# The first layer of a four-layer network, rewritten as pipelines of two batches

## The chip, the cores and the metric

The kernel runs on one core of a Trainium2 chip. The metric is the time of one execution on the device in microseconds; lower is better. The engines are called as in the profile: PE (TensorE, matmuls; PEld are its weight loads), DVE (VectorE), ACT (ScalarE), POOL (GpSimd) and SP (SyncE, which here only issues DMAs). Everything is computed in 32-bit floats.

## The reference

A residual stream x of 8 batches of 512 tokens and width 128 runs through four layers. Each layer is a half feed-forward, an attention and the same half feed-forward again, each with a layer norm in front:

```
x = x + 0.5 * ffn(layernorm(x));  x = x + attn(layernorm(x));  x = x + 0.5 * ffn(layernorm(x))
```

The change is in layer 0. Its feed-forward is a mixture of 8 experts for 4096 tokens: softmax over 8 logits (router weights), the two largest kept, 7 experts with a capacity of 512 tokens each (the first 512 in token order; relu between a 128x512 and a 512x128 matrix), and the eighth a copy of the input times its weight. Its attention works inside segments of 32 tokens without heads (scores over all 128 columns, scale 1/sqrt(8)). Beside it the first tokens of the 16 segments of a batch attend to one another; their result is added to every token of its segment before the output matrix:

```
fused = softmax(Q K^T * scale) V  +  softmax(Qg Kg^T * scale) Vg  (one row for a segment)
out   = fused @ wc.T + bc
```

Layer 1's feed-forward (the spline step, with an own norm inside) opens the next layer, and the change also moves how it starts. Layers 2 and 3 have small feed-forward weights that are worked out inside the kernel from 8 gathered matrices (l2_ffn_weights) and from the products of 8 pairs of matrices (l3_ffn_weights).

## The kernel before

x lives in SBUF, 8 tiles of 128 x (4 x 128), one for each batch of 512 tokens. Layer 0 goes stage by stage, each over all eight batches:

1. norm: stats takes bn_stats and bn_aggr of all 32 pieces on DVE, one square root on ACT and a refinement on DVE; DVE scales all pieces (L190), PE turns them (L193), ACT copies them (L194).
2. router (L330), the two largest and the routing table: the rank of each token within its expert comes from matmuls with triangular matrices, and the table of which token sits in which row of which expert from one-hot products on DVE (L440 to L443, four chunks of eight tiles) and PE (L445). The table goes through seven small DMAs (L453) to give src and dst, the row numbers for gather and scatter.
3. The experts: POOL issues indirect DMAs that gather rows of xn from DRAM (fetch, L489) and scatter the results to DRAM (put, L493); PE transposes, multiplies (L505, L513), ACT and DVE apply relu and copy. POOL's order is written by hand: put(e - 2) and fetch(e) in turns. yd, where the results go, is filled with zeros at the start of the kernel, from ACT's DMA queue.
4. back: the two result rows of each token are read from yd (r) and added with their weights on DVE (L539).
5. l3_ffn_weights and l2_ffn_weights work out later layers' weights.
6. l0_attn: norm again, projections of all batches (L564, L575), the summary attention for all batches, then per batch scores (L619), softmax_t, the local product (L626), its sum with the summary (L629), the output matrix (L634) and the addition to x.
7. norm, router, table, experts once more, and then back through l1_start.

l1_start is a pipeline with places: plan and a dictionary todo put each step of a batch at a place n, and the steps are then emitted in order of place; within tc.manual_schedule the order on the engines that it names is the order of emission, and each engine's queue is worked off in that order. A place is not a time: an engine goes on to its next instruction as soon as that one's inputs are there. Engines that are not named (POOL and SP in most places) are ordered by the framework's scheduler. In l1_start the norm of each batch is measure (bn_stats on DVE, then some 13 small operations on POOL with a power of -0.5) and four scalings on ACT (L833), followed by turned (four transposes on PE and a copy on ACT), and the steps of layer 1's feed-forward for batches 0 and 1, from place 13 and from place 33. whiten is measure plus four scalings on POOL (L231). The attention of layer 1, l1_block, follows; its projections (L909) need the turned batch 0 at the end of l1_start, and its buffers are cleared on POOL (L881, L884, L889).

## Time and profile before

| | us |
|---|---|
| median of 3 runs | 3029.14 (3025.25 to 3033.32) |
| profiled execution, its own time | 3021.69 |
| profiled execution, its span from first to last instruction | 3019.9 |
| PE busy | 2626.2 (87%) |
| DVE busy | 1985.9 (66%) |
| ACT busy | 1691.9 (56%) |
| POOL busy | 839.8 (28%) |
| mean granted PE clock | 0.92 of full |
| layer 0 and the start of layer 1 (to the first projection of layer 1) | 621.5 |

The busy times are of one execution and sum an engine's instructions, whatever waited for them. A busy PE is not PE at its peak: a matmul at half clock is busy for twice as long. Waits are listed by who waited and whose end released it; a wait at an engine that is not needed costs nothing. Which engine sets the pace is to be read stage by stage, since layer 0 is made of stages with different limits and the other layers are long pipelines.

### The profile page before, as it was taken

The numbers are of one execution on the slowest core, as the hardware profiler recorded it, in microseconds if no ns is written. First come the engines' busy times: TensorE is split into PE (matmuls) and PEld (weight loads), VectorE is DVE, ScalarE is ACT, GpSimd is POOL, SyncE is SP. The second block draws the span as 40 slices with busy tenths as digits, with TensorE's granted clock in tenths as the row PEclk, the third lists the DMA queues.
The fourth block names the chain that finished last, engine by engine and source line by source line (L and its number), as shares of the span: only waits on it lengthen the run. The fifth ranks groups of instructions, "written<-read, shape, count | busy, mean of one in ns | idle before, by whom it ended". The sixth has DMA issues, their size and how long they took to land.

```text
span 3019.9 us, 50759 instructions
## 1 busy us (share of the span) xinstructions
PE 2626.2 (87%) x18608; PEld 1512.7 (50%) x18608; DVE 1985.9 (66%) x5383; ACT 1691.9 (56%) x4102; POOL 839.8 (28%) x1783
## 2 busy tenths in 40 slices
PE   3637665669999999889999999999999999999997
PEld 3425543323334333456565565565555555555554
DVE  5345542458888877354756656655578888888886
ACT  1002101405555555566666665666488888888884
POOL 0433035722222233134254353351221011100100
PEclk9877577559999999899999999999999999999998
DMA  5031002100100000000000000000000000000000
GB/s 181 27 94 47 29 21 68 36 15 17 24 21 19 16 16 2 32 1 1 1 1 1 1 1 1 1 1 1 15 15 2 19 15 19 5 19 19 16 5 8
DMA packets 65863, 62.92 MB, mean 21 GB/s; under 512 B 9544, under 2 KB 55760, under 8 KB 63920
## 3 DMA queue, kind: packets, MB, share of 16 engines
q1 hardware_dynamic: 58144, 42.75, 5.5%
q10 hardware_dynamic: 3344, 8.99, 0.8%
q0 software_dynamic: 4128, 7.94, 0.8%
q8 instruction: 148, 2.42, 0.3%
q14 instruction: 99, 0.81, 0.1%
HBM read 36.83 MB, written 22.87 MB: 20 GB/s over the span
## 4 chain that ended last, share of the span: by engine, by line
PE 60%; DVE 14%; ACT 9%; POOL 8%; issue 5%; DMA 4%; SPq 0%; POOLq 0%; DVEq 0%; ACTq 0%
PE s L1080 8%; PE tp L1112 7%; PE s L934 5%; PE o L964 4%; PE yp L300 4%; PE o L1369 4%; PE o L1132 4%; PE s L1320 3%; ACT e L1327 3%; PE tp L1346 3%; DVE nm L935 3%; PE s L954 2%; PE pp L1289 2%; PE op L1383 2%; PE vp L1302 2%
## 5 line engine op out<-in xcount | busy, mean ns | idle before, releaser
L1084 DVE TENSOR_REDUCE nm<-s 128x2 f32<-128x1024 f32 x256 | 312.8, 1222 | 105.6 <-PE s L1080 105.2
L935 DVE TENSOR_REDUCE nm<-s 128x2 f32<-128x1024 f32 x256 | 307.6, 1219 | 105.9 <-PE s L954 82.6
L1091 ACT ACTIVATE e<-s,nm 128x512 f32<-128x512 f32 x512 | 350.4, 702 | 29.4 <-DVE nm L1084 29.4
L956 ACT ACTIVATE pr<-s 128x512 f32<-128x512 f32 x512 | 274.4, 600 | 143.6 <-PE s L954 142.8
L204 POOL TENSOR_TENSOR d<-st 128x4 f32<-128x4 f32 x88 | 17.9, 204 | 1200.4 <-DVE rs L1097 600.6
L1120 ACT ACTIVATE p<-tp 128x512 f32<-128x512 f32 x512 | 275.5, 608 | 71.1 <-PE tp L1112 69.1
L954 PE MATMUL s<-q,k 32*128 32x512 f32 x1024 | 309.7, 638 | 3.7 <-DVE at L977 2.3
L934 PE MATMUL s<-k,q 32*128 32x512 f32 x1024 | 290.5, 671 | 25.8 <-DMA k<-sk 14.3
L1080 PE MATMUL s<-k,q 32*128 32x512 f32 x1024 | 291.9, 648 | 4.8 <-ACT e L1091 2.4
L1112 PE MATMUL tp<-cst,e 128*128 128x128 f32 x2048 | 287.0, 282 | 5.8 <-DVE e L1104 5.0
L1327 ACT ACTIVATE e<-e,m 128x512 f32<-128x512 f32 (+3 forms) x512 | 285.6, 568 | 8.1 <-DVE m L1324 8.0
L1112 PEld LDWEIGHTS tp<-cst,e 128*128 128x128 f32 x2048 | 220.9, 142 | 136.8 <-issue 100.6
L1324 DVE CUSTOM_DVE_ANT_0 e<-s,bias 128x512 f32<-128x512 f32 (+3 forms) x512 | 219.9, 486 | 99.9 <-PE s L1320 99.4
L1348 ACT COPY pt<-tp 128x512 f32<-128x512 f32 x320 | 173.7, 588 | 100.7 <-PE tp L1346 100.3
L1104 DVE TENSOR_SCALAR e<-e,rs 128x512 f32<-128x512 f32 x448 | 201.9, 487 | 9.1
L303 DVE SCALAR_TENSOR_TENSOR x<-yp,sel,x 128x128 f32<-128x128 f32 x512 | 178.4, 349 | 22.6 <-PE yp L300 8.2
L231 POOL TENSOR_SCALAR xn<-x,sm,rs 128x128 f32<-128x128 f32 x232 | 188.7, 824 | 6.2
L1320 PE MATMUL s<-qk 64*128 64x512 f32 (+3 forms) x1024 | 174.6, 460 | 2.3 <-DVE m L1324 1.6
L1346 PE MATMUL tp<-cst,e 128*128 128x128 f32 x1280 | 169.1, 278 | 1.7 <-ACT e L1327 1.7
L1346 PEld LDWEIGHTS tp<-cst,e 128*128 128x128 f32 x1280 | 141.4, 142 | 41.6 <-issue 16.1
L1377 DVE TENSOR_TENSOR att<-o,rt 128x512 f32<-128x512 f32 x64 | 44.3, 692 | 173.3 <-ACT rt L1376 173.3
L934 PEld LDWEIGHTS s<-k,q 32*128 32x128 f32 x1024 | 88.2, 193 | 132.6 <-DVE nm L935 74.9
(423 smaller groups left out, 4816.3 us busy)
## 6 DMA issues: line engine op xcount, KB each, us to landing
r<-yd SPq DMA_DIRECT2D x32, 256.0 KB
yd<-zero ACTq DMA_DIRECT2D x4, 1024.0 KB
xd<-xn SPq DMA_DIRECT2D x16, 256.0 KB
k<-sk SPq DMA_DIRECT2D x64, 64.0 KB
sk<-pu SPq DMA_DIRECT2D x16, 256.0 KB
w<-in_l_w SPq DMA_DIRECT2D x14, 256.0 KB
q<-sq SPq DMA_DIRECT2D x32, 72.0 KB
x<-in_x SPq DMA_DIRECT2D x8, 256.0 KB
```

The costliest lines, as they stand in the source:

```text
L934: nc.tensor.matmul(s[:, jj, :], lhsT=q[cut, g, i * P : (i + 1) * P], rhs=k[cut, g, :], start=True, stop=True)
L935: nc.vector.tensor_reduce(nms[b, g // 2][:, i, 2 * h : 2 * h + 2, g % 2], s, AX.X, ALU.max, negate=True)
L954: nc.tensor.matmul(s, lhsT=k[cut, g, kt * P : (kt + 1) * P], rhs=q[cut, g, :], start=True, stop=True)
L956: nc.scalar.activation(e, s, AF.Exp)
L1080: nc.tensor.matmul(s[:, jj, :], lhsT=q[cut, g, i * P : (i + 1) * P], rhs=k[cut, g, :], start=True, stop=True)
L1084: nc.vector.tensor_reduce(nm, scores[n, h], AX.X, ALU.max, negate=True)
L1091: nc.scalar.activation(e, s[:, jj, :], AF.Exp, bias=nm[:, jj : jj + 1], accum_out=sm[:, jj : jj + 1])
L1112: nc.tensor.transpose(tp[:, kt, :], probs[n][j][:, kt * P : (kt + 1) * P], self.ident)
L1120: nc.scalar.activation(p, tp, AF.Exp)
L1320: nc.tensor.matmul(s[:, jj, 0:w], lhsT=qs[n][cut, i * P : (i + 1) * P], rhs=ks[n][cut, 0:w], start=True, stop=True)
L1327: outs.append(lambda e=e, jj=jj: nc.scalar.activation(e, e, AF.Exp, bias=mins[n][:, jj, i : i + 1], scale=-1.0, accum_out=sums[n][:, jj, i ...
L1346: nc.tensor.transpose(tp[:, k, :], block(n, jj, i, kt), self.ident)
```

## The change

Layer 0 is written anew as l0_block, five stretches with the order of PE, ACT and DVE written by hand:

- **Start**: four pairs of batches, pair(g) at place 6g. A pair is a measure of two batches together (POOL's small operations on 8 columns instead of 4), and for each of the two a scaling on ACT 7 places later, turned 3 places after that, and logits one after that. The choice of the two largest is made in two halves (chosen).
- **Table and experts**: the one-hot work in eight chunks of four tiles; the zeros for yd are written from SP's queue, from a tile cleared on POOL, behind the table in program order. Fetches run three experts ahead, put(e) comes after expert e, and fetch(e + 3) goes in turns with it. An expert is split in turn, inner and outer, with turn(e + 1) between inner(e) and outer(e). Beside the first pass of experts the eighth expert's part is added to x, and layer 3's products and layer 2's sums are made in pieces between the experts; layer 2's gathers are issued ahead of the first table, with their small loads on ACT's queue.
- **Middle**: returned results are loaded and added batch by batch, 10 places apart; pair(g) is measured at place 20g + 13, its attention begins at 20g + 34, and its second norm, with the router's logits, at 20g + 49. From the first addition to the last logits a pair takes 62 places, and a pair starts every 20.
- **Attention**: wv and wc are multiplied once to one matrix (wvc), so that there is no output matmul: leave accumulates the local product and, through a 0/1 matrix own, the summary's row of each segment straight into the output. The biases bv and bc are added to x as one row, bc + 2 bv wc. The softmax works on the unscaled scores, with the scale in the exponential. The summary is made per pair.
- **Second table and experts**, as the first, without the weights beside them.
- **Start of layer 1**: additions 4 places apart, pairs at 8g + 6, and the feed-forward steps of batches 0 and 1 side by side, two places a step, from places 20 and 21; whiten(0) at 55 and its transposes at 61.

stats, norm, router, l0_ffn, l0_attn and l1_start are gone. l3_ffn_weights and l2_ffn_weights return lists of steps. Layers 1 to 3 are as before. The core of the diff:

```diff
-            self.norm(ps)
-    def norm(self, ps, tag="mm", bufs=None):
...
+    def pair(self, todo, g, n, bank, gap, *also):
+        nc, got = self.nc, []
+        def scale(k):
+            (nb, rs), b = got[0], 2 * g + k
+            for i in range(4):
+                t = 4 * k + i
+                nc.scalar.activation(self.xn[b][:, i, :], self.x[b][:, i, :], AF.Identity, bias=nb[:, t : t + 1], scale=rs[:, t : t + 1])
...
+        at(n, lambda: got.append(self.measure([self.x[2 * g], self.x[2 * g + 1]], True)))
+        for k in range(2):
+            b = 2 * g + k
+            at(n + gap + 2 * k, lambda k=k: scale(k))
+            at(n + gap + 3 + 2 * k, lambda b=b: self.turned(self.xn[b], bank, self.xt[b]))
+            for delay, work in also:
+                at(n + gap + 3 + 2 * k + delay, lambda b=b, work=work: work(b))
...
+                for k in range(8):
+                    ts = slice(4 * k, 4 * k + 4)
...
-            with tc.manual_schedule(engines={mybir.EngineType.Pool}):
-                for e in range(9):
-                    if e < 7:
-                        for s in range(4):
-                            if e >= 2:
-                                put(e - 2, s)
-                            fetch(e, s)
-                        expert(e)
...
+                with tc.manual_schedule(engines={*FIXED, mybir.EngineType.Pool}):
+                    for e in range(3):
+                        for s in range(4):
+                            fetch(e, s)
+                    turn(0)
+                    for e in range(7):
+                        inner(e)
+                        if e < 6:
+                            turn(e + 1)
+                        outer(e)
+                        for s in range(4):
+                            put(e, s)
+                            if e + 3 < 7:
+                                fetch(e + 3, s)
+                        for k, work in enumerate(beside):
+                            if k * 7 // len(beside) == e:
+                                work()
...
+                def leave(k):
+                    x, op = self.x[2 * g + k], bank("op", (P, 4, P))
+                    for i in range(4):
+                        s0 = 16 * k + 4 * i
+                        nc.tensor.matmul(op[:, i, :], lhsT=box["own"][:, 32 * s0 : 32 * s0 + P], rhs=soft["go"], start=True, stop=False, skip_group_check=True)
+                        for j in range(4):
+                            rows = slice(32 * j, 32 * j + 32)
+                            nc.tensor.matmul(
+                                op[rows, i, :], lhsT=soft[k][rows, 32 * i : 32 * i + 32], rhs=vs[k][rows, i, :], start=False, stop=True, skip_group_check=True)
+                    nc.vector.tensor_tensor(x, x, op, ALU.add)
+                for k in range(2):
+                    at_(n + 2 * k, project, k, 0)
+                    at_(n + 2 * k, project, k, 1)
+                    at_(n + 2 * k + 1, values, k)
+                    at_(n + 3 + 2 * k, score, k)
+                    at_(n + 4 + 2 * k, powers, k)
+                    at_(n + 6 + 2 * k, divide, k)
+                    at_(n + 10 + 2 * k, leave, k)
+                at_(n + 4, summary)
+                at_(n + 5, powers, 2)
+                at_(n + 7, divide, 2)
+                at_(n + 9, spread)
...
+                    for g in range(4):
+                        self.pair(todo, g, 6 * g, bank, 7, (1, logits))
+                    chosen(todo, 0, 20)
+                    chosen(todo, 1, 33)
...
+                    w2, more = self.l2_ffn_weights(self.keep, pool)
...
+                    table(wk)
+                    z = wk.tile([P, 4, 512], F32, tag="h", name="z")
+                    nc.gpsimd.memset(z, 0.0)
+                    for n in range(4):
+                        nc.sync.dma_start(out=self.yd[2048 * n : 2048 * n + 2048, :].rearrange("(p n) d -> p (n d)", p=P), in_=z.rearrange("p a b -> p (a b)"))
...
+                    experts(wk, ps, [weights, *(work for works in zip(parts, steps, more(ps)) for work in works), more(ps)[8]])
...
+                    for b in range(NB):
+                        at(todo, 10 * b - 20, load, b)
+                        at(todo, 10 * b, add, b, 0)
+                        at(todo, 10 * b + 2, add, b, 1)
+                    for g in range(4):
+                        n = 20 * g + 13
+                        self.pair(todo, g, n, bank, 7)
+                        attention(todo, g, n + 21, wk, ps, bank)
+                        self.pair(todo, g, n + 36, bank, 7, (1, logits))
+                    chosen(todo, 0, 84)
+                    chosen(todo, 1, 123)
...
+                    experts(wk, ps, [weights] + [lambda b=b: self_part(b) for b in range(NB)])
...
+                    for b in range(NB):
+                        at(todo, 4 * b - 16, load, b)
+                        at(todo, 4 * b, add, b, 0)
+                        at(todo, 4 * b + 1, add, b, 1)
...
+                        self.pair(todo, g, 8 * g + 6, bank, 6, (1, lambda b, heads=heads, hts=hts: hts.__setitem__(b, heads[b % 2][0](self.xt[b]))),
+                                  (3, lambda b, heads=heads, hts=hts: heads[b % 2][1](hts[b])))
+                    for b in range(2):
...
+                        n = 20 + b
+                        self.plan(todo, [n + 2 * k for k in L1F_TAIL], *self.l1_ffn_steps(b, w1, bank, twin, self.xn[b], self.xt[b]))
+                    n = 21 + 2 * L1F_TAIL[-1]
+                    self.plan(todo, (n, n + 6), lambda _: self.whiten(0, self.xn[0]), lambda xn: self.turned(xn, bank, self.xt[0]))
```

## The prediction

> **What bounds the kernel now.** I read the busy times cut by stage first, with the cuts put where one stage hands over to the next in the timeline: start, first routing table, first experts, the stretch with the attention (the middle), second table, second experts, the start of layer 1, and the rest. Columns: window, length, busy time (instructions) of PE, PEld, DVE, ACT, POOL, then the granted PE clock, DMA share and GB/s.
>
> ```profile
> 0.00:61.30 61.30, 21.66 (x96) 19.15 (x96) 28.22 (x140) 7.89 (x12) 4.01 (x10) 1.00 0.70 223
> 61.30:99.20 37.90, 19.72 (x74) 16.03 (x74) 30.62 (x70) 0.00 (x0) 0.00 (x0) 0.93 0.01 1
> 99.20:198.30 99.10, 66.78 (x308) 41.44 (x308) 14.53 (x21) 12.46 (x21) 54.76 (x56) 0.84 0.11 37
> 198.30:372.20 173.90, 101.68 (x884) 82.03 (x884) 107.15 (x415) 27.23 (x56) 23.38 (x41) 0.63 0.22 64
> 372.20:409.60 37.40, 19.48 (x74) 15.87 (x74) 30.81 (x70) 0.00 (x0) 0.00 (x0) 0.73 0.01 0
> 409.60:511.30 101.70, 66.04 (x308) 41.09 (x308) 14.53 (x22) 12.46 (x21) 54.51 (x56) 0.85 0.12 41
> 511.30:621.50 110.20, 56.49 (x168) 33.89 (x168) 60.95 (x197) 38.56 (x79) 67.81 (x169) 0.50 0.16 49
> 621.50:3019.90 2398.40, 2274.38 (x16696) 1263.24 (x16696) 1699.08 (x4453) 1593.27 (x3913) 635.35 (x1451) 0.97 0.04 10
> ```
>
> The first seven rows are layer 0 with the start of layer 1: 621.5 us in which no engine is busy for more than 67% of a window but DVE in the tables (81%). The last row is not touched by the change and has PE busy for 95%. So the change can win or lose only in 621.5 us, by overlap. The waits and the timeline say why each window is as long as it is:
>
> ```profile
> 14.39 11.84 ACTq L390 DMA_DIRECT2D yd<-zero  x4
> 27.56 0.23 ACT L171 ACTIVATE sd<-ve 128x32 f32<-128x32 f32 x1
> ...
> 117.58 1.00 POOL L493 DMA_INDIRECT yd<-y,dst  x1 [8.35 <-ACT y L515]
> ...
> POOL x L635 <- DVE xn L190: 41.5, 7, 37.4
> PE pp L1475 <- DVE st L166: 37.0, 1, 37.0
> ACT xt L194 <- PE pt L193: 36.2, 12, 15.3
> ...
> ACT xn L833 <- POOL sm L220: 21.1, 2, 19.1
> ```
>
> At the start ACT is held for 11.84 us issuing the zeros, so the square root runs at 27.56 though its input was there at 18.3. In the experts the POOL queue, which issues all gathers and puts, stands still for 8.35 us until the first result. In the middle PE waits 37.0 us in one piece while DVE adds and measures all eight batches, and ACT, POOL and PE each wait for the whole stage ahead. Before layer 1 ACT waits 19.1 us for a norm on POOL, which was then clearing layer 1's buffers (L881 to L889).
>
> **The Trainium skill.** "TensorE: Matmul & The Clock Gate", Part 1: the PE clock is halved unless the array has been busy for a window of about 3.4 us. The trace agrees and adds that small matmuls don't count for much: clock 1.00 at 262 to 288 in dense projections, 0.50 at 295 to 385 though PE was busy for 93% of 300 to 325. "SBUF — State Buffer", SBUF: two separate sides: DVE operations with two SBUF inputs and POOL operations lock each other out. The trace agrees: eight L539 additions took 2.2 us with POOL idle (208 to 220) and 3.57 us at 524.6 with POOL at work. "ScalarE: Activation LUTs", What ACT_TABLE_LOAD costs: each switch of set costs a load; the trace has 1283 ns each.
>
> **The change, stage by stage** (window before to window after).
>
> *Start, 61.3 to 51.* Removed: the root, its table load, 32 aggregates (0.17 us), 32 DVE scalings; the zeros leave ACT. Added: four norms of two batches, each 8 statistics on DVE (0.22 us in a row, 1.8), 13 POOL operations (4.1 us for four columns at 530.06 to 534.15; eight columns are not shown, bounds 4.1 and 5.5, I take 4.6), and on ACT 4 scalings (1.65) and a copy (0.59) a batch. PE needs 1.1 + 1.9 = 3.0 a batch for transposes and logits at half clock. If the first statistics start at 5 (x lands at 4.7), PE begins at 5 + 1.8 + 4.6 + 1.7 = 13 and ends after 8 x 3.0 = 24 at 38; the second half of the choice, 20 operations of 0.31 on 128 columns and an exponential, takes 6.7: 45. If DVE must first do layer 1's weights, whose data land at 14.1 (L662), all is 11 later: 56. I take 51.
>
> *Tables, 37.9 to 37 and 37.4 to 34.5.* Cutting the one-hot work into 8 chunks (2.06 us of DVE each, by halving L443, L440, L441) lets PE start 2 us earlier and end 1.6 after DVE instead of 3.3; the self parts that DVE mixed in are gone. That is 3 us each. In the first, 5 small DVE operations and a matmul for the fused weights come ahead of it: +2. SP gets the four zero transfers (11.84 us of issue on ACT before) ahead of or beside the table's v transfers: nothing if they go early in the 37 us, up to +12 if they are queued in front; I take 0. The nine gathers of l2_ffn_weights (1.3 us each on POOL) lie in the same idle 37 us; their four loads on ACT have the choice in front of them as cover.
>
> *Experts, 99.1 to 95 and 101.7 to 94.* Three experts are fetched ahead, so the loop no longer waits for put before fetch. Start to first put stays 19. Then POOL: four rounds of put and fetch of 8 x 1.28 = 10.3, three of puts alone at 2.5 (each waits for the one before, 1.5 us in the trace) = 10: 71, + 2.2 to land = 92. PE per expert: 3.9 + 0.8 + 4.1 = 8.8, under POOL's 10.3, in the second pass: 92 to 96. In the first pass each expert also carries a layer 3 product (1.13, eight in all) and some 4 DVE additions: 10.0 to 11.5, so either may bound: 92 to 102.
>
> *Middle, 173.9 to 145.* What leaves: layer 3 and layer 2 weights, 25 us almost bare (222 to 250). PE work per batch, at half / full clock: two sets of transposes 2.2 / 1.6; q and k 3.0 / 2.0 (0.744 at L909, 1.98 for four at L564); values 2.05 / 1.1; scores 0.66 / 0.4; leave, 8 matmuls on own (0.256 / 0.135) and 32 small ones (a quarter of that if four run side by side as L964's do, half as bound) 4.1 / 2.2, up to 6.1; logits 1.9 / 1.1. Sum 13.9 / 8.4, and 1.2 / 0.7 a pair for the summary: 116 / 70 in all. DVE: per pair 16 additions 4.6, two norms 3.5, softmax 3.1, leave 1.4, summary 1.8, gaps 1.6 = 16; with the first choice 70 in all. ACT 13.6 a pair, 54. POOL 13 a pair, 52. PE sets the pace. It starts at 2.7 (first return, 198.3 to 200.98) + 4.6 + 1.8 + 4.6 + 1.7 = 15.5, and in front of the last logits waits once for an addition, a norm and a scaling, 9. With 116: 15.5 + 116 + 9 + 6.7 for the choice = 147; with 70 and 10 more in the first pair: 111. A third warm gives 135; 10 for PE standing in its fixed order behind a younger pair's transposes makes 145. A pair takes 62 places and starts every 20, so three do overlap.
>
> *Start of layer 1, 110.2 to 102.* The two spline chains go side by side instead of 20 places apart. DVE: 32 for both chains, 8 x 2.7 additions, 7 norms; PE 60 at half clock. First scores at 29, DVE-bound to 72, then on POOL two whitenings of 7.5 and a third for batch 0, additions and transposes: 100. POOL's clearing (6 x 1.8, 8 DMA issues of 0.55) moves and may land in front of that last whitening, +15, or wholly beside it; 2 for it.
>
> Sum after: 51 + 37 + 95 + 145 + 34.5 + 94 + 102 = 558.5, that is 63 less than 621.5. Against the profiled execution (3021.7, of which 3019.9 span) that is 2959; the median of the runs shown is 7.4 above this execution, so the forecast is **2966**. Layers 1 to 3 keep their 2398.4, give or take 5.
>
> **Rivals.**
> 1. *PE stays warm in the middle.* For: the projections and values of a pair are 8 us of dense matmuls, and 4.9 us of transposes were enough at 255. Against: logits and small products kept it at 0.50 for 90 us. Middle 111: 2932. Chance 0.23.
> 2. *Small gain.* DVE starts behind layer 1's weights (+5), zeros queued in front of the table (+12), clearing on POOL in front of the last whitening (+13): 2996. For: all three are placed by the scheduler, and the stall of 19.1 us shows the last. Chance 0.20.
> 3. *Slower: the written order makes PE and DVE take turns in the middle.* Each place is fixed on three engines; if leave waits for a softmax that stands on DVE behind additions waiting for r, and DVE then waits for PE, their times add: 15.5 + 116 + 70 + 9 + 6.7 = 217, 72 more than I take, 3038. It decides from a middle of 208 us. Against: ten places lie between values and leave. Chance 0.12.
> 4. That pairs don't overlap, since PE is full with two: this is the forecast's own cold case, 2968.
>
> **Numbers.** Forecast 0.45. A measurement here can tell 0.3% (9 us) from no change. Faster: forecast, rival 1 and most of rival 2: 0.84; same 0.05; slower 0.11. The range: below, rival 1 with the early start (2932 less 6) and the experts' good ends (less 6), rounded to 2915; above, rival 2 with the experts' bad end, 3012.
>
> **What would show it.** Right: PE's first transposes at 11 to 15; no ACT issue of zeros; POOL pairs of put and fetch without a break after the first 18 us of experts; middle 135 to 155 with PE busy for over 70% of it and DVE under 60%; in layer 1's start no wait of ACT for POOL over 8. Wrong: a middle over 170, PE waiting for DVE in many pieces of 1 to 3 us there, or layer 1's first projection over 110 after the last put.

## The result, and the profile after

Not faster but slightly slower: **3036.35 us** (median of 18 runs, 3030.52 to 3040.17) against 3028.85 us (18 runs) for the kernel before on the same chip, a ratio of 1.0021 (95% interval 1.0014 to 1.0027). The forecast was 2966, with a range to 3012. The profiled execution took 3030.52 us with a span of 3028.6, 8.7 more than before.

The busy times of the kernel after, cut where one stage hands over to the next, as they were for the kernel before (window, length, busy time and count of PE, PEld, DVE, ACT, POOL, granted PE clock, DMA share, GB/s):

```profile
0.00:59.80 59.80, 24.10 (x100) 20.41 (x100) 19.67 (x90) 18.69 (x44) 20.15 (x66) 1.00 0.72 226
59.80:96.30 36.50, 20.45 (x74) 15.29 (x74) 23.21 (x45) 0.00 (x0) 9.90 (x9) 0.95 0.17 46
96.30:199.80 103.50, 70.22 (x374) 49.08 (x374) 28.05 (x73) 14.58 (x29) 54.92 (x56) 0.83 0.22 67
199.80:374.40 174.60, 114.52 (x826) 70.96 (x826) 69.90 (x262) 51.73 (x118) 50.08 (x145) 0.59 0.13 37
374.40:409.20 34.80, 18.64 (x72) 14.05 (x72) 22.37 (x42) 0.00 (x0) 0.00 (x0) 0.79 0.01 0
409.20:507.90 98.70, 62.44 (x308) 41.38 (x308) 25.30 (x61) 12.17 (x21) 54.77 (x56) 0.79 0.14 42
507.90:623.70 115.80, 54.00 (x168) 34.06 (x168) 60.99 (x202) 34.03 (x76) 62.62 (x128) 0.51 0.16 46
623.70:3028.60 2404.90, 2277.51 (x16696) 1263.62 (x16696) 1696.34 (x4447) 1594.06 (x3914) 631.18 (x1437) 0.97 0.04 10
```

| stage | before | forecast | after | after less forecast |
|---|---|---|---|---|
| start, to the first mask | 61.3 | 51 | 59.8 | +8.8 |
| first table | 37.9 | 37 | 36.5 | -0.5 |
| first experts | 99.1 | 95 | 103.5 | +8.5 |
| middle | 173.9 | 145 | 174.6 | +29.6 |
| second table | 37.4 | 34.5 | 34.8 | +0.3 |
| second experts | 101.7 | 94 | 98.7 | +4.7 |
| start of layer 1, to its first projection | 110.2 | 102 | 115.8 | +13.8 |
| the rest | 2398.4 | 2398.4 | 2404.9 | +6.5 |

The column of differences sums to 71.7. So the question is not one loss but where five stages lost what they were to gain, and why a part that was not touched got longer. Four things are to be seen in the trace.

At the start POOL works on two pairs in turns, with a clearing between (timeline of POOL; start, duration, instruction, in brackets the idle time before it and its releaser):

```profile
10.08 0.25 POOL L170 TENSOR_TENSOR d<-st 128x8 f32<-128x8 f32 x1 [7.24 <-DVE st L167]
...
12.37 1.80 POOL L700 MEMSET z<- 128x2048 f32 x1
...
16.32 3.28 POOL L176 TENSOR_TENSOR r<-ve,half 128x8 f32<-128x8 f32 x2
...
20.83 0.37 POOL L185 TENSOR_TENSOR sm<-sm,rs 128x8 f32<-128x8 f32 x2
```

The first measure begins at 10.1, since a pair waits for its second batch of x, and ends at 21, which is 11 us later and not 4.6: its steps alternate with those of pair 1 (every "x2" is one of each), and the 1.8 us memset of the zeros' source lies in between.

In the middle, what PE waited for (total, times, longest; 33.3 of the first row is the wait for the stage to begin). vp L635 is the summary attention, which works on firsts, the first token of each segment, copied together by POOL; gp L646 (spread in the code) makes the summary's rows, for which leave then waits; pt are the transposes of a norm, lp the logits:

```profile
PE pt L225 <- ACT xn L207: 41.1, 2, 33.3
PE vp L635 <- POOL firsts L595: 14.6, 4, 7.0
PE lp L392 <- ACT xt L227: 7.6, 8, 1.8
PE gp L646 <- DVE t L629: 4.7, 1, 4.7
```

The tail of layer 0, on POOL: the last whitening, which the first transposes of layer 1 wait for, alternates with the clearing of layer 1's buffers and takes from 605.1 to 622.5; PE stands for 36.0 us in front of those transposes (from 584.2).

```profile
603.34 1.80 POOL L966 MEMSET q<- 128x2048 f32 x1 [1.73 <-issue]
605.11 0.20 POOL L170 TENSOR_TENSOR d<-st 128x4 f32<-128x4 f32 x1
...
605.55 1.80 POOL L969 MEMSET k<- 128x2048 f32 x1
...
611.37 1.05 POOL L176 TENSOR_TENSOR r<-ve,half 128x4 f32<-128x4 f32 x1
...
619.39 3.14 POOL L196 TENSOR_SCALAR xn<-x,sm,rs 128x128 f32<-128x128 f32 x4
```

And 600 us further on, in layer 1, ACT has a hole that the kernel before doesn't have:

```profile
1238.66 0.33 ACTq L1586 DMA_DIRECT2D wp<-in_l_attn  x1
1239.04 0.60 ACT L1041 ACTIVATE pr<-s 128x512 f32<-128x512 f32 x1 [7.43 <-DVE bq L1591]
```

ACT does exponentials for layer 1 there. In the order of its queue the load of a weight of layer 3 (wp) comes next, and it is issued only at 1238.66. What ended the wait is a DVE instruction behind the last step of a spline (1237.8 to 1238.5); my reading is that wp's tile lies in memory that this spline still uses, which no run shows by itself. PE then waited 6.9 us for ACT.

### The profile page after: what moved, and what is told of

Same layout as the page of the kernel before. It is cut to its first block, busy times and chain, and to the rows that moved or that the text cites. A ratio compares the mean times of both kernels' runs of the same rounds, so it can differ in the third digit from the quotient of the medians.

```text
span 3028.6 us, 50809 instructions
## 1 busy us (share of the span) xinstructions
PE 2641.9 (87%) x18618; PEld 1508.9 (50%) x18618; DVE 1945.8 (64%) x5220; ACT 1725.3 (57%) x4202; POOL 883.6 (29%) x1896
## 4 chain that ended last, share of the span: by engine, by line
PE 55%; DVE 9%; ACT 8%; POOL 5%; issue 2%; DMA 0%; POOLq 0%; ACTq 0%; DVEq 0%
PE s L1165 8%; PE tp L1197 7%; PE s L1019 5%; PE o L1049 4%; PE yp L286 4%; PE o L1459 4%; PE o L1217 4%; PE s L1410 3%; ACT e L1417 3%; PE tp L1436 3%; DVE nm L1020 3%; PE s L1039 2%; PE pp L1379 2%; PE op L1473 2%; PE vp L1392 2%
## 5 line engine op out<-in xcount | busy, mean ns | idle before, releaser
L170 POOL TENSOR_TENSOR d<-st 128x4 f32<-128x4 f32 (+1 forms) x96 | 19.9, 207 | 1272.9 <-DVE st L167 672.4
L1019 PE MATMUL s<-k,q 32*128 32x512 f32 x1024 | 291.2, 671 | 22.1 <-DVE nm L1020 11.5
L1414 DVE CUSTOM_DVE_ANT_0 e<-s,bias 128x512 f32<-128x512 f32 (+3 forms) x512 | 219.9, 486 | 99.0 <-PE s L1410 98.5
L225 PE MATMUL pt<-cst,xn 128*128 128x128 f32 x360 | 81.4, 347 | 156.1 <-ACT xn L207 99.0
L1410 PE MATMUL s<-qk 64*128 64x512 f32 (+3 forms) x1024 | 174.6, 460 | 2.6 <-DVE m L1414 1.9
L1436 PEld LDWEIGHTS tp<-cst,e 128*128 128x128 f32 x1280 | 141.4, 142 | 41.6 <-issue 16.1
```

The source lines that it names most:

```text
L1019: nc.tensor.matmul(s[:, jj, :], lhsT=q[cut, g, i * P : (i + 1) * P], rhs=k[cut, g, :], start=True, stop=True)
L1410: nc.tensor.matmul(s[:, jj, 0:w], lhsT=qs[n][cut, i * P : (i + 1) * P], rhs=ks[n][cut, 0:w], start=True, stop=True)
L1436: nc.tensor.transpose(tp[:, k, :], block(n, jj, i, kt), self.ident)
```

## The experiments

Times are given as ratio to the kernel before in the same comparison, since the chips differed: the kernel before took 3021.6, 3024.4, 3036.0 and 3023.6 us in the four comparisons. The kernel after stands at 1.0021. Stage lengths are from the profiles; layer 2, the same code in all, took between 921.8 and 935.1 us in them, so that only the stage that an edit touches is compared.

### Layer 3's loads off ACT's queue

```diff
-        nc.scalar.dma_start(out=self.wp, in_=a["l3_attn"])
+        nc.sync.dma_start(out=self.wp, in_=a["l3_attn"])
```
(and the same for wv)

> The kernel after the change, with layer 3's two weight loads wp and wv (L1586, L1588) issued on SP's queue instead of ACT's. Between the last scores of layer 1 (1206.3 us) and the first scores of layer 3 (2190.7 us) the changed kernel is 10 us longer than the one before, though the code there is the same. Theory: ACT stands for 7.4 us at 1231.6 to 1239 in front of the issue of wp, whose memory is only free when DVE has added the spline result (1238.5); PE then waits 6.9 us for ACT and runs cold for 12 us. With the issue on SP the wait is nobody's: time falls by 8 to 10 us, to about 3027, and the waits of ACT for DVE bq and of PE for ACT pr (6.9 us) are gone. Rival: PE and ACT are held there by the spline chain itself (DVE and POOL) and the issue only shows the wait: no change (within 2 us).

Measured: 1.0009 (1.0000 to 1.0018). The waits are gone, and layer 1 takes 639.8 us from its first projection to layer 2's first instead of 645.1 (before: 638.1). The theory holds for the wait; of the 8 to 10 us that it promised 5.3 show in layer 1, and 3.6 in the ratio. In every kernel here with this edit layer 1 took 635.2 to 640.5 us, in every other one made from the changed kernel 645.1 to 651.0. The change had left that code as it was; that the places of tiles in memory made the wait is argued, not shown.

### Layer 1's clearing off POOL

```diff
-                nc.gpsimd.memset(q, 0.0)
+                nc.vector.memset(q, 0.0)
...
-                    nc.gpsimd.dma_start(out=k[32 * j + 8 : 32 * j + 9], ...)
+                    nc.sync.dma_start(out=k[32 * j + 8 : 32 * j + 9], ...)
```

> The kernel after the change, with layer 1's clearing taken off POOL: the six memsets of q, k and va (1.8 us each) on DVE, the eight k<-in_one transfers on SP. Theory: at 603 to 623 us POOL alternates between the 13 small steps of the last whitening (batch 0) and this clearing, so that the whitening takes 20.3 us (605.1 to 622.5) with PE, ACT and DVE idle; alone such a measure takes 4.2 us and the four scalings 3.1. First projection of layer 1 then comes about 10 to 12 us earlier (610 to 614 instead of 623.7), time 3025 to 3028. Rival: the start of layer 1 is set by the rope table and the q, k buffers, which have to be loaded and cleared after the spline work has given its memory back (603.3), so that the first scores (641.1) do not move by more than 3 us and the time neither.

Measured: 1.0004 (0.9994 to 1.0013). The start of layer 1 takes 100.3 us instead of 115.8, and the first scores come at 628.7 instead of 641.1. That is what the theory asked for (its 605.1 to 622.5 are 17.4 us, not 20.3); the whole run shows about 5 us of it.

### Dense work in front of leave

```diff
                     for i in range(4):
                         s0 = 16 * k + 4 * i
+                        for _ in range(3):
+                            nc.tensor.matmul(op[:, i, :], lhsT=wa[:, 0, :], rhs=wa[:, 1, :], start=True, stop=True, ...)
```

> The kernel after the change, with three additional 128 x 128 x 128 f32 matmuls (of the q and k weights, results thrown away by the next matmul) ahead of each of the 32 own matmuls of leave. Theory: the PE clock stays at half through leave because its matmuls are small (32 rows, 32 columns), though PE is busy without a break for 10 us; the additions are dense, 0.27 us each at half clock. They cost 26 us if the clock stays at half (middle 200). If they bring the clock up, leave takes (1.30 + 0.8) / 2 = 1.05 a step instead of 1.30 and the transposes, logits and projections after it run at full clock: middle 150 to 165 and time 3011 to 3027. Rival: the clock is not what holds the middle, since the waits between PE, ACT and POOL have their own length: middle 180 to 200, time 3042 to 3062.

Measured: 1.0191 (1.0171 to 1.0212). The middle, in the same columns as above:

```profile
197.40:415.00 217.60, 156.44 (x1018) 110.17 (x1018) 69.93 (x262) 51.78 (x118) 50.31 (x145) 0.59 0.10 30
```

PE's busy time rose by 42 us and the middle by 43: **PE paces the middle**, every microsecond of work added in front of leave shows. The additions cost 42 and not the theory's 26, since each of these matmuls stands in the profile as two instructions of 0.27. The clock stayed at 0.59, so the theory that these additions lift it is wrong. PE was busy from 234 to 256 without a break, for more than half of that with matmuls on 128 rows (the additions and transposes), and the clock stayed at 0.50:

```profile
234.00:256.00 22.00, 22.00 (x127) 15.56 (x127) 0.69 (x1) 0.59 (x1) 0.21 (x1) 0.50 0.06 17
```

### A burst of wide matmuls in front of leave

```diff
                     x, op = self.x[2 * g + k], bank("op", (P, 4, P))
+                    for _ in range(5 if k == 0 else 0):
+                        nc.tensor.matmul(op.rearrange("p i d -> p (i d)"), lhsT=wa[:, 0, :], rhs=qk[0, 0], ...)
```

> The kernel after the change, with five additional 128 x 128 x 512 f32 matmuls in front of the first leave of each pair (results overwritten). The three dense 128-column matmuls ahead of each own matmul did not bring the clock up, though they and leave kept PE busy for 21 us; the projections, 512 columns wide, do so in 3 to 4 us. Theory: only long streams count, so the clock is at 1.00 after the third addition, and the leave steps behind it take 0.65 us instead of 1.30 until it falls back after 4 to 6 us: additions 7 us, gain 4 to 6 us a pair, middle 175 to 182. Rival: what holds the clock down is the waiting before, not the width: the burst stays at half clock (1.7 us each), middle 200 or more.

Measured: one run, 3046.81 us, beside 3035.95 for the kernel before. The steps of leave on PE, first in the kernel after, then with the burst (timeline of PE; own is L655 in the first and L657 in the second):

```profile
236.32 0.79 PE L655 MATMUL op<-go,own 32*128 32x128 f32 x2 [1.74 <-DVE go L648]
237.04 0.65 PE L658 MATMUL op<-v,t 32*32 32x128 f32 x8
```

```profile
231.66 5.79 PE L654 MATMUL op<-qk,wat 128*128 128x512 f32 x10
237.38 0.48 PE L657 MATMUL op<-go,own 32*128 32x128 f32 x2
237.79 0.42 PE L660 MATMUL op<-v,t 32*32 32x128 f32 x8
...
244.08 1.98 PE L592 MATMUL pp<-xt,wat 128*128 128x512 f32 x4
...
255.21 0.31 PE L635 MATMUL vp<-firsts 128*32 128x32 f32 x2 [4.73 <-POOL firsts L595]
```

Own fell from 0.79 to 0.48 and the local product from 0.65 to 0.42. The clock went to 1.00 during the burst and stayed there through all 8 steps and the transposes between, 6.7 us without a pause, and the next pair's projections (1.98 instead of 3.78); it fell back in PE's 4.73 us wait for firsts, at 254.8. The middle was 176.2: the bursts cost about what they brought (four of 5.8 to 6.5 us, 24 in all, and PE's busy time was 114.5 us with them as without).

The theory put the rise down to the width of the matmuls, and two other stretches speak against that. In the kernel before, 28 transposes of 128 columns in a row took the granted clock from 0.50 to 1.00, at 257.5. In the kernel after, 60 score matmuls of layer 1, 512 columns wide but on 32 rows, kept PE busy without a break, and the clock stayed at 0.50 (timeline before, timeline after, and the busy times of the second stretch):

```profile
254.02 5.58 PE L193 MATMUL pt<-cst,xn 128*128 128x128 f32 x28 [1.27 <-DVE bh L1249]
```

```profile
641.10 26.78 PE L1019 MATMUL s<-k,q 32*128 32x512 f32 x60 [10.55 <-DMA k<-sk]
```

```profile
641.10:667.80 26.70, 26.70 (x60) 8.48 (x60) 17.15 (x14) 0.00 (x0) 0.00 (x0) 0.50 0.01 1
```

So it is not the number of columns. Runs of matmuls on all 128 rows raised the clock; matmuls on 32 rows each, alone or in turns with those on 128, did not. That the rows decide fits all four stretches, but no run changed the rows alone.

### The second norm later

```diff
-                        self.pair(todo, g, n + 36, bank, 7, (1, logits))
+                        self.pair(todo, g, n + 40, bank, 7, (1, logits))
```
(and chosen at 88 and 127)

> The kernel after the change, with the second norm of each pair in the middle four places later (n + 40 instead of n + 36, and the two choices 4 later). Theory: in the written order the scaling of pair g's second norm (place 20g + 56) stands on ACT in front of the second q and k copies of pair g + 1 (also place 20g + 56), and the norm has only begun when leave of pair g was done three places earlier. ACT waits for POOL (up to 6.8 us), the summary matmul on PE then waits for the copies of firsts (3.5, 3.5 and 7.0 us). With four places more these waits of 14 us go: middle 160 to 163 instead of 174.6, time 3021 to 3025. Rival: PE paces the middle at half clock (114 us busy) and the norm only comes due later; what is gained in the middle of a pair is lost at its end, where the logits then wait for the norm: under 4 us.

Measured: 1.0064 (1.0042 to 1.0086), the middle 180.5. A miss. PE's waits there:

```profile
PE pt L225 <- ACT xn L207: 56.9, 7, 32.7
PE lp L392 <- ACT xt L227: 10.2, 6, 3.1
```

The wait for firsts is gone, as promised, but the wait for the scaled xn has grown from 41.1 us in 2 to 56.9 in 7: PE now stood before the second norm's transposes, in front of the next pair's spread and leave. A wait on a norm that can only begin after leave isn't moved away by placing the whole norm a little later; its transposes have to stand behind other work.

### The second norm's transposes behind the next leave

```diff
-                        self.pair(todo, g, n + 36, bank, 7, (1, logits))
+                        self.pair(todo, g, n + 36, bank, 13, (1, logits))
```
(and chosen at 90 and 129)

> The kernel after the change, with the second norm measured where it was (n + 36), but its scalings, transposes and logits six places later (gap 13 instead of 7; choices at 90 and 129), that is behind or between the leave steps of the next pair. With the norm four places later as a whole the wait moved: PE stood 3.3, 2.8 and 3.1 us in a pair for the scalings, in front of the next pair's spread and leave. Theory: the second norm runs on DVE, POOL and ACT for 12 us after leave while PE has 9 us of projections, values and scores; wherever its transposes stand in front of the next leave, PE waits. Behind it they wait for nobody: PE's waits of 14.6 us for firsts and 7.6 us for xt in front of logits go, middle 155 to 162 instead of 174.6, time down by 10 to 17 us against the changed kernel. Rival: PE then waits at the same rate for DVE's softmax (spread and leave), which the norm's statistics have covered so far: under 5 us.

Measured: 0.9993 (0.9984 to 1.0002), the middle 164.3, 10 us less than after. PE's waits:

```profile
PE pt L225 <- ACT xn L207: 37.0, 4, 31.7
PE gp L646 <- DVE t L629: 13.1, 4, 4.7
...
PE vp L635 <- POOL firsts L595: 1.4, 1, 1.4
```

The firsts cost 1.4 instead of 14.6 us. The rival has a part too: 13.1 us for the softmax in front of spread, where the norm's transposes had been.

### The ten places taken back

```diff
-                        attention(todo, g, n + 21, wk, ps, bank)
-                        self.pair(todo, g, n + 36, bank, 7, (1, logits))
+                        attention(todo, g, n + 11, wk, ps, bank)
+                        self.pair(todo, g, n + 26, bank, 7, (1, logits))
```
(and chosen at 74 and 113)

> The kernel after the change, with attention and second norm of each pair ten places earlier (n + 11 and n + 26, choices at 74 and 113), so that two pairs are under way in the middle instead of three; all else as it is. Theory: the middle is paced by PE at half clock plus waits of PE for the second norm, which comes before the next pair's summary in either order; the ten places only change which transposes fill PE's waits. The middle stays within 168 to 182 us (174.6 with the ten places). Rival: the ten places are what fills the pair's own waits; without them PE waits for values, softmax and norm of one pair at a time: middle over 190, time up by more than 15 us.

Measured: 0.9990 (0.9978 to 1.0003), the middle 164.6. Neither the theory nor the rival had this: with two pairs under way instead of three the middle is 10 us *shorter*. PE waited 4.3 us for firsts instead of 14.6; behind its first transposes its waits fell by 5.8 us in all, and its own work by 4.0. So the third pair, as placed by the change, costs 10 us.

### POOL in the written order at the start

```diff
-            with tc.manual_schedule(engines=FIXED):
+            with tc.manual_schedule(engines={*FIXED, mybir.EngineType.Pool}):
                 with tc.tile_pool(name="f0a", bufs=4, space=PSUM) as ps:
+                    z = pool.tile([P, 4, 512], F32, tag="z", name="z")
+                    nc.gpsimd.memset(z, 0.0)
...
-                    z = wk.tile([P, 4, 512], F32, tag="h", name="z")
-                    nc.gpsimd.memset(z, 0.0)
```

> The kernel after the change, with POOL also in the written order in the first stage and the zeros' source cleared ahead of it, in a tile of its own. Theory: the first pair's measure takes from 10.1 to 20.9 us instead of the 4.6 forecast, because POOL's order alternates between the steps of pairs 0 and 1 and has the 1.8 us memset of z between them. In the written order pair 0's measure ends at 15 to 16, PE's first transposes come at 16 to 17 instead of 21.6, the first mask at 54 to 55 instead of 59.8: time 3023 to 3026 where the changed kernel has 3030. Rival: the pace of scaling, transposes and logits (7.0 us a pair, ACT and PE taking turns) or the arrival of x sets the end of the stage: it shortens by less than 2 us.

Measured: 1.0000 (0.9989 to 1.0011). PE's first transposes come at 15.6 instead of 21.6 and the mask at 53.8 instead of 59.8, as the theory said. And something it had not said: the start of layer 1 takes 109.0 instead of 115.8, because the clearing now runs 55 us earlier, beside the spline (POOL's first and last memset of layer 1):

```profile
547.74 1.81 POOL L966 MEMSET q<- 128x2048 f32 x1 [2.13 <-DVE m L875]
...
563.13 1.79 POOL L974 MEMSET va<- 128x2048 f32 x1
```

The new tile moves the others in memory, and layer 1's buffers seem to fall on places that are free sooner; the clearing is as early in every later kernel with this tile, but the layout was not tried by itself.

### The edits together

Four edits in one kernel: layer 3's loads, the clearing on DVE and SP, POOL's order at the start, the transposes behind the next leave.

> The kernel after the change with four edits together: layer 3's weight loads on SP, layer 1's clearing on DVE and SP, POOL in the written order at the start, and the second norm's scalings, transposes and logits six places later. If the causes are separate the stages add up: start 59.8 to 53.8, middle 174.6 to 164, start of layer 1 115.8 to 101, layers 1 to 3 down by 5: 36 us less in the profile than the changed kernel, that is 0.99 of the kernel before. Rival: the clearing and the start share a cause (with the zeros' tile moved, the clearing ran early by itself and the start of layer 1 took 109.0), and the layers after give back what layer 0 gains: 20 us less at most, 0.995.

Measured: 0.9939 (0.9923 to 0.9956). Start 53.8 and middle 164.8, as alone, but the start of layer 1 114.2, not 101: the rival. With the zeros' tile the clearing is early anyway (537 to 552), and now it stands on DVE, in front of the spline steps that the tail waits for.

The same with two pairs in the middle (attention at n + 11, the second norm at n + 26 with gap 13, chosen at 80 and 119):

> As the four edits together, but with two pairs under way in the middle (attention at n + 11, second norm at n + 26 with its scalings six places later) instead of three. Theory: the ten places are not needed, since PE paces the middle (110 to 112 us busy, clock 0.6); with two pairs and the scalings behind the next leave the middle is 155 to 163, at or under that of the three pairs. Rival: with two pairs values, scores and softmax of one pair follow each other without other work between, so that PE waits for the softmax: 165 to 172.

Measured: 0.9956 (0.9939 to 0.9972), the middle 173.2. The rival holds, PE waits for one pair's softmax and projections:

```profile
PE gp L646 <- DVE t L629: 14.1, 4, 4.3
PE op L655 <- DVE go L648: 6.5, 4, 2.1
...
PE pp L592 <- ACT xt L227: 6.1, 4, 3.2
```

The two ways to be rid of the waits don't add. With the transposes behind the next leave the third pair pays (164.8 against 173.2), without it two pairs are better (164.6 against 174.6).

The four edits with the pairs of the first stage every four places instead of six:

```diff
-                        self.pair(todo, g, 6 * g, bank, 7, (1, logits))
+                        self.pair(todo, g, 4 * g, bank, 7, (1, logits))
```

> As the four edits together, with the pairs of the first stage every four places instead of six (choices at 18 and 27). Theory: ACT has the scalings of the next pair behind the copy of this pair's second batch, which waits 2.9 us for transposes behind logits; so each pair takes 7.05 us where PE has 6.0. With four places the next scaling stands in front of that copy: 6.0 to 6.3 a pair, the start 3 us shorter than with six places (51 instead of 54). Rival: POOL, with 4.6 us a pair and all four pairs' measures in a row, or x's arrival is due as late: no change.

Measured: 0.9925 (0.9908 to 0.9942), the start 52.0 instead of 53.8: a gain, of 1.8 us rather than 3.

And this with the clearing back on POOL:

> The kernel after the change with four edits: layer 3's weight loads on SP, POOL in the written order at the start, the second norm's scalings six places later, the first stage's pairs every four places; layer 1's clearing stays on POOL. Theory: with the zeros' tile in a place of its own the clearing already runs early, beside the spline work (547 to 569 us), so that moving it to DVE brought nothing and cost DVE 11 us there (start of layer 1 112 to 114 instead of 109). Back on POOL: start of layer 1 108 to 110, 3 us under the kernel with the clearing on DVE. Rival: the clearing lands in front of the last whitening again: 115 or more.

Measured: 0.9913 (0.9889 to 0.9937), the start of layer 1 109.2 (112.2 with the clearing on DVE), the clearing at 536 to 553 on POOL. The theory holds.

### The waits of PE filled

```diff
+    def warm(self, bank, n):
+        t = bank("wm")
+        for _ in range(n):
+            self.nc.tensor.matmul(t, lhsT=self.ident, rhs=self.cst[:, 0:512], start=True, stop=True)
...
                 def spread():
+                    self.warm(bank, 4)
...
+                        if g == 3:
+                            at(todo, n + 51, self.warm, bank, 4)
```

> As the four edits with the clearing on POOL, with four 128 x 128 x 512 f32 matmuls of constants (results read by nobody) in front of each pair's spread, where PE waits 1 to 5 us for the softmax, and four in front of the last pair's second transposes. Theory: the clock falls back only in PE's pauses, and no small matmul brings it up again; if the pauses are filled, leave, transposes and logits run at 1.00 throughout: a pair takes 24 instead of 32 us, the middle 130 to 145 instead of 164, clock over 0.85, time 20 to 30 us less than without. This is the forecast's term of the clock (a third warm) measured by itself. Rival: with PE warm the chain of softmax and norm on DVE, POOL and ACT sets the pair's period, and the additions only lie in front of leave: 155 to 170.

Measured: 0.9895 (0.9871 to 0.9918). The middle without and with the additions:

```profile
191.20:357.20 166.00, 114.20 (x826) 70.52 (x826) 68.50 (x262) 53.25 (x118) 50.17 (x145) 0.58 0.14 39
```

```profile
188.30:345.40 157.10, 121.61 (x866) 70.91 (x866) 68.84 (x262) 53.03 (x118) 50.18 (x145) 0.70 0.14 41
```

From 166 to 157 us, the clock from 0.58 to 0.70: a smaller gain than the theory's 130 to 145, which took the clock to hold. It doesn't:

```profile
278.35 3.70 PE L223 MATMUL wm<-cst 128*128 128x512 f32 x8
...
286.81 0.42 PE L664 MATMUL op<-v,t 32*32 32x128 f32 x8
287.16 1.87 PE L230 MATMUL pt<-cst,xn 128*128 128x128 f32 x8
289.41 1.87 PE L397 MATMUL lp<-rw,xt 128*128 128x8 f32 x8 [0.37 <-ACT xt L232]
291.21 0.79 PE L661 MATMUL op<-go,own 32*128 32x128 f32 x2
291.93 0.65 PE L664 MATMUL op<-v,t 32*32 32x128 f32 x8
```

The additions end at 282.0 and the first half of leave runs at full clock (0.42 for the local product); in the second half the same instructions take 0.79 and 0.65. The pause of 0.37 us between them is not the cause. The eight transposes ahead of it are slow already, and the clock had fallen at 287.3, in work without a break (busy times as above):

```profile
283.90:287.30 3.40, 3.40 (x42) 2.00 (x43) 0.00 (x0) 3.40 (x10) 1.59 (x2) 1.00 0.29 82
287.30:289.00 1.70, 1.70 (x8) 1.33 (x7) 0.69 (x1) 1.70 (x6) 1.06 (x2) 0.50 0.00 0
```

So the other half of the theory, that the clock falls only in PE's pauses, is wrong as well: here 3.4 us filled almost wholly by the small matmuls of leave were enough, where in the run with the burst the clock outlived 6.7 us of them. What makes the difference stays open. In all sixteen traces of this case the granted clock keeps each value for a whole number of periods of 3.41 us (here 1.00 for four of them, to 287.31), so a change can't be put down to the pause that happens to stand beside it. The 157 us lie in the rival's range, but its chain is not shown as the pace: PE was busy for 121.6 of them, and behind its first transposes stood for only 11.5 us in waits for data up to the last logits.

Ten more at the start and ten before layer 1's first scores:

```diff
+                    at(todo, -1, self.warm, bank, 10)
...
+                    self.plan(todo, (n - 6, n - 6, n - 6, n - 6), *enter[2:], lambda _: self.warm(bank, 10))
```

> As before, with ten such matmuls ahead of the first transposes (PE has nothing to do until 15.6 us) and ten behind layer 1's first values, where PE waits 10.9 us for the k transfer. Theory: first stage at full clock, limited by ACT (4.4 us a pair) and POOL (4.6): start 46 to 48 instead of 52; the first 60 scores of layer 1, 27 us at half clock, become limited by DVE (15 maxima of 1.25): 19 us. Together 10 to 14 us less than with the middle alone. Rival: the clock falls in ACT's and DMA's pauses all the same: under 4 us.

Measured: 0.9882 (0.9862 to 0.9903), 2986.23 us; the start took 51.7 us where it had been 52.4, and the first 60 scores 26.79 us, as without. So the two stages gain 0.7 us, as the rival has it:

```profile
15.97 0.95 PE L230 MATMUL pt<-cst,xn 128*128 128x128 f32 x4
18.60 1.06 PE L397 MATMUL lp<-rw,xt 128*128 128x8 f32 x8 [1.68 <-ACT xt L232]
...
22.10 1.88 PE L397 MATMUL lp<-rw,xt 128*128 128x8 f32 x8 [1.96 <-ACT xt L232]
```

The first transposes and logits run at full clock (0.95, then 1.06); the clock falls at 20.4, as PE waits for ACT's copies for the second time, and the next logits take 1.88. In layer 1 it falls at 604.0, 1.1 us into the scores. The intervals of this kernel and the two before it overlap, so that the steps between them are read from the stages alone. This one beats both kernels: 1.2% under the kernel before, 1.4% under the one after (0.9882 / 1.0021).

## Why the prediction was wrong

**Right.** The tables (36.5 and 34.8 for 37 and 34.5), the zeros on SP (issued at 46 to 51, ahead of the table's transfers at 89: nothing, as taken), the first put 19 us into the experts (96.3 to 115.2), PE as the pace of the middle, the first transposes there after 16.5 us (15.5). The first pair's statistics did not stand behind layer 1's weights.

**Wrong, the middle, +29.6, three terms.**

- PE's work, +10.5: 114.5 us where the sum had 104 (116 at half clock, less 12 for "a third warm"). The step that failed is the price of leave, "4.1 / 2.2, up to 6.1" a batch: it took 5.2 (four steps of 1.30, all at half clock), 41.6 us for eight batches instead of 32.8, +8.8. The rest of PE's work took 72.9 us where 83.2 at half clock were priced: 10.3 less, since projections, values and scores ran in part at full clock, close to the 12 that were taken for it. So 114.5 lies near the cold sum of 116 by luck. A clock of 1.00 is what a faster middle would need, and filling PE's waits brought only part of it; but the clock was not the main error of this term. "TensorE: Matmul & The Clock Gate", Part 1, of the Trainium skill has the clock follow busy and idle windows of about 3.4 us; the periods agree (3.41 us), but in these traces busy was not enough to raise it (0.50 at 234 to 256 in the run with dense work) nor to keep it (it fell at 287.3 after 3.4 us without a break).
- The waits, +17.8. 10 for the fixed order and 9 at the end were taken; between the first transposes and the last logits (216.3 to 367.6) PE stood 36.8 of 151.3 us. 14.6 are the firsts: a second norm runs on DVE, POOL and ACT for 12 us after leave (248.0 to 260.3) while PE has 9 us of projections, values and scores, and its scaling stands on ACT in front of the copies that the summary needs. The prediction asked only whether leave waits for a softmax, not what the norm after leave holds up. Shown by moving it (the middle 10 us shorter) and by taking the ten places back (10 us shorter, 4 of them PE's own work).
- 1 us at the beginning.

"So three do overlap" is right, and it brought nothing: since PE is full, a third pair can only fill PE's waits, and placed as it was it made some.

**Wrong, the start of layer 1, +13.8.** The step is "2 for it", with a bound of 15: the clearing did land in front of the last whitening. Without it the stage took 100.3, against 102 forecast. The view for it was there, the 19.1 us wait for POOL of the kernel before; rival 2 had it at its right size (+13).

**Wrong, the start, +8.8.** PE began at 21.6 instead of 13. "x lands at 4.7" is the first batch, but a pair needs the second, at 9.1 (+4.4); and the measure of 4.6 us was taken as if POOL did one at a time. It took 11; in the written order PE began 6 us earlier, and the stage was 6 us shorter. A lone measure of eight columns took 5.2 (210.5 to 215.7). Then the eight batches took PE 31.4 us (21.6 to 53.0) instead of "8 x 3.0 = 24": that price left out PE's waits for ACT's copies, 7.9 us in all (+7.4). Taking 51 between the two cases 45 and 56 covered part of this (and 13 and 24 make 37, not 38).

**Wrong, the experts, +8.5 and +4.7.** The rounds of put and fetch were taken at 10.3 us from two issues of 1.28. The first four took 52.8 us (115.2 to 168.0), 13.2 each; in the second pass 46.9, 11.7 each. What POOL waited for in the first pass:

```profile
POOL yd L514 <- DMA yd<-y,dst: 28.1, 16, 2.8
```

18.5 of these 28.1 us lie in the last three rounds, which were charged 1.5 a put for it. The other 9.6 are five puts of the first four rounds that waited for the put before them even with a fetch between; nothing was charged there. The rest of the loss in these rounds is shorter waits of several kinds. This is read from the trace; no run tried it, and the same first pass took 98.5 to 104.6 us in the other kernels.

**Wrong, the rest, +6.5.** "Layers 1 to 3 keep their 2398.4, give or take 5" assumed that equal code has equal waits. Moving wp's load gave 5.3 back.

**The rivals.** The third, slower, has the right side and nearly the time (3038), but by chance: the middle was 174.6, far from its 208, and PE did not take turns with DVE (66% busy, DVE 40%). The second had one of its three parts. The first, a warm middle, is out (clock 0.59). The fourth, that PE is full with two pairs, had the mechanism, though not its 2968: two pairs did better than three. By its list of signs the forecast was wrong where it said it would be: the middle over 170 and the first projection more than 110 us after the last put.

One reading of the prediction is wider than its page. "SBUF — State Buffer", SBUF: two separate sides, of the Trainium skill lets DVE operations with two SBUF inputs collide only with POOL operations that read SBUF. The trace fits that: of the eight additions at 524.6 a single one was long, 1.23 us instead of 0.35, and it stood beside a POOL addition (L808, 1.26 us).

**What stays open.** The whole runs show less than the stages (12.4 us earlier scores, 5 us in the ratio, for the clearing); the spread of single runs and of layer 2 between profiles covers it, but no run settles it.

## What to carry to other kernels

A list of work per engine gives a bound; in an order written by hand the time comes from chains through the other engines, so for each instruction placed ahead of others ask how long its inputs take from the last thing they need, and put it behind work that lasts as long. An engine whose order is left to a scheduler mixes urgent and idle work; count every idle job that can become ready beside an urgent chain as if it stood in front of it. And equal code is not equal time: a load that waits held up the whole queue that issued it, here 7.4 us on ACT, in code that nobody had touched; look for such waits behind any change of the memory's layout.

## What the runs showed of the hardware

- PE's clock, up: runs of matmuls on 128 rows raised it, of 512 columns (five of them, 5.8 us) or of 128 (28 transposes, at 257.5 in the kernel before, 3.5 us into them). 26.7 us of unbroken matmuls on 32 rows with 512 columns left it at 0.50, and so did 22 us of 128-row and 32-row ones in turns.
- PE's clock, down: small matmuls held it for 6.7 us in one run and lost it in another after 3.4 us, both without a pause. In all sixteen traces it kept each value for whole multiples of 3.41 us.
- On POOL the power of -0.5 took 1.67 us for 128 x 8 and 1.04 for 128 x 4; every other operation of the measure took about 0.2 for either.
